# Layer 0's first expert prepared between row blocks, split rank gathers, and another memory order for layer 1

## The chip, the cores and the metric

The kernel runs on one core of one Trainium2 chip. A core has five engines with queues of their own: TensorE (PE in the profile: matrix products; PEld is its weight load), VectorE (DVE), ScalarE (ACT), GpSimd (POOL) and SyncE (SP, which here only issues transfers). They meet through semaphores. Transfers run on 16 DMA engines that all queues of the core share. The metric is the device time in microseconds (us) of one execution, as the median of several runs. All data are float32.

## The reference

The input `x` has 32 batches of 128 x 1024. Two residual layers follow each other.

```python
# layer 0
h = einsum('bct,bcd->bdt', x, weights[cond])        # weights[cond[b]]: 128 x 128, per batch
logits = h @ gate_w.T                               # 4096 tokens of 1024, 64 experts
w, sel = top_k(softmax(logits), 8); w = w / sum(w)
# token -> slot: the first 256 tokens of each expert, in token order, the rest dropped
out = (silu(xin @ wg) * (xin @ wu)) @ wd            # per expert 256 x 1024 -> 384 -> 1024
x = x + sum over the chosen experts of w * out
# layer 1
c = x @ W.T + scal[a] * (x @ A[a].T) @ Bm[a].T      # a = adapter of the batch, rank 16
logits = c @ router_w.T + router_b                  # 8 experts
gate = top 2 of softmax(logits), made to sum to 1
y = c @ base_w.T + base_b + 2 * sum_e gate_e * (c @ lora_A[e]) @ lora_B[e]
x = x + y
```

## The kernel before

**Three stages.** Stage A (0 to 200 us) makes `h`, the routing and part of a weight product. Stage B (259 to 2123 us) runs over the 64 experts. Stage C (2123 us to the end) is layer 1, over 16 pairs of batches. Between A and B and between B and C lie the row blocks of the weight product.

**Stage A.** The loop runs over the 32 batches `b`. `loaded_batch(b)` gathers the batch's matrix `w_b` (indirect DMA on GpSimd's queue) and loads `x_b` (0.5 MB, SyncE's queue); six batches are loaded ahead, in buffers of a pool with six of each. `mixed` makes `ph` (16 matmuls of 128 columns) and `as_rows` and `stored` write it as token rows to `hbuf` in DRAM. `logits` makes `plog` (16 matmuls of 64 columns, four batches to a PSUM bank), `topped`, `powers` and `weights_of` choose the eight experts and their weights. For a group of four batches, `counted(g)` makes `pcnt` (how many tokens of each batch go to each expert), adds it up over the batches in `upto` (four VectorE additions), then makes two tiles `prk` (a token's rank in its batch and its weight) that ScalarE copies and stores to `ranks` in DRAM. `plog`, `pcnt` and `prk` share a PSUM pool, `pa_sm`, with three buffers. `carried(b)` copies `x` of a batch to `ybuf` in DRAM, on SyncE's queue; after the loop it is called again for the last eight batches.

**The weight product.** Layer 1 never forms `c`: the matrix W (and the adapters' Bm) is multiplied with the head, which is lora_A, router_w and base_w side by side, 1160 columns in three blocks of 388, 388 and 384 (`BLOCKS`, n = 0, 1, 2). `combined(n, d)` or `multiplied(n, d)` makes one of nine row blocks d of a column block, `pcw`, with eight matmuls; its right factor is `hw` (`head_block(n)`), its left one of three tiles of three row blocks each (`left_block`, tiles `WB_a` and `WB_b`). These share the buffers of the experts' weights: `hw_n` those of `wg`, the `WB` tiles those of `wu` and `wd`. Row blocks 0 to 7 of n = 0 and 1 go to `cwbuf` in DRAM, block 8 to `G_sb`. n = 0 is made inside stage A, n = 1 between A and B, n = 2 between B and C.

**From ranks to tokens.** `looked_up(es)` computes, for four experts, which batch holds each of the 256 slots (`batch`, `rank`, `row`: eleven VectorE operations). `fetched(part, count)` gathers `count` rows of `ranks` into `rkg`, one indirect DMA each (two per expert). `found(part, lo, hi)` finds each slot's token and weight (`slot_tok`, `slot_w`) and `byq`; `placed` multiplies `byq` by `spread` on TensorE (`prow`, one PSUM bank in the pool `pf`) and writes `slot_row`, the rows of `hbuf`. `gathered(e)` issues eight indirect DMAs into `xin`. `columns(e)` transposes `xin` to `xT` on VectorE. `prow`'s pool has one bank, and it is not used before the row blocks of n = 1.

**Stage B.** Gate and up product of an expert are one 256 x 1024 times 1024 x 768 product in the Winograd form: seven products of half size (`product`, tile `pp`, four matmuls each) of sums of quarters (`weight_sums`: tiles t1, t2, t4 and one in place; `token_sums`: s1, s2, s4 and one in place), with their results added on VectorE (`gated`). `turned` transposes h on TensorE (`pth`, copied to `hTb`), `po` is the down product, ScalarE scales it into `o_sb`, and GpSimd scatters it with an addition into `ybuf`. The sums and the tokens of expert e + 1 are made while expert e runs.

**Passage to C and stage C.** The map `BM` (10 x 2 x 512 columns on each partition) is loaded from `cwbuf` (two of three pieces, `PIECES`), from `lora_B`, from `G_sb` and from the row blocks of n = 2. `with_ones` adds 1 on the diagonal, so that the residual x is part of the product; it compares `chan` (a row 0 to 1023) with `own`. `map_sums(lo, hi)` makes the sums ts1, ts2, ts4 for the seven-product form, `token_sums2` those of the tokens (ss1, ss2, ss4). `loaded_x1` loads a pair's tokens from `ybuf` (`xq`), which needs the last scatter; `turned_x1` transposes them on VectorE to `X`. `inner` makes `px`, the product of `X` with the first 136 columns and the adapter's columns (`pxw`); `routed`, `corrected` and `turned_in` make the expert and adapter rows of `X`. Then `pr_c` are the seven products of a pair.

**What sets the order.** The objects `dve`, `pe`, `act`, `pool` and `sync` record instructions that keep the order of the program on their engine; instructions issued through `nc.` are placed by a scheduler. Tiles of a pool with one buffer that follow another pool on the same addresses wait for the last readers of what lay there:

```python
    c1 = ctx.enter_context(tc.tile_pool(name="c1", bufs=1, reuse_waits="tile"))
    BM = c1.tile([P, KC, 2, 512], F32, name="BM")
    pxw = [c1.tile([P, HC, NA], F32, name=f"pxw_{i}") for i in range(2)]
    chan = c1.tile([P, 2, 512], F32, name="chan")
```

In this order `BM` lies over the tables of slots and the last `o_sb` tiles of stage B.

Of the kernel before, what the change touches and what calls it, by code (L numbers as in the profile page):

```python
# [51 lines left out]
def kernel(  # L52
# [273 lines left out]

    with (
# [3 lines left out]
        tc.tile_pool(name="pa_big", bufs=4, space=PSUM) as pa_big,  # L331
        tc.tile_pool(name="pa_sm", bufs=3, space=PSUM) as pa_sm,
# [3 lines left out]
        def loaded_batch(b):  # L336
# [8 lines left out]
            sync.dma_start(xs[b].rearrange("p j c -> p (j c)"), x_q[b])  # L345
# [78 lines left out]
        def counted(g):  # L424
            mask, wt = masks[g], wts_of[g]
            pcnt = pa_sm.tile([P, GB, E], F32, name=f"pcnt_{g}", tag="sm")
# [103 lines left out]
        part = {0: looked_up([0, 1, 2, 3])}  # L530
        fetched(part[0], 4 * NJ)
        for b in range(NB - 8, NB):
            carried(b)
        gathers = {}
        for d in range(HC + 1):
            step = combined(1, d)
            next(step)
            if d == 2:
                found(part[0], 0, 1)
                placed(part[0])  # L540
                gathers[0] = gathered(0)
            elif d == 3:
                found(part[0], 1, 2)
                placed(part[0])
                gathers[1] = gathered(1)
            elif d == 4:
                found(part[0], 2, 4)
                part[1] = looked_up([4, 5, 6, 7])
                fetched(part[1], 4 * NJ)
            next(step)  # L550

# [4 lines left out]
    dve.tensor_scalar(adapter_rows, adapter_i, float(P), pcol, ALU.mult, ALU.add)  # L556
    dve.tensor_copy(adapter_f, adapter_i)
    dve.tensor_tensor(
        smask,
        adapter_f.unsqueeze(2).to_broadcast([P, NB, E2]),  # L560
        iota_t[:, 0:E2].unsqueeze(1).to_broadcast([P, NB, E2]),
        ALU.is_equal,
    )
    dve.tensor_tensor(
        smask, smask, scal_bc.unsqueeze(1).to_broadcast([P, NB, E2]), ALU.mult
    )

    dve.tensor_scalar(own, iota_t[:, 0:HC], float(Q), inquad, ALU.mult, ALU.add)
    dve.tensor_scalar(far, quad, float(W4), None, ALU.mult)
    dve.tensor_scalar(own, own, far, None, ALU.add)  # L570

    nc.sync.dma_start(rb_bc, router_b.to_broadcast([P, E2]))


    with (
# [3 lines left out]
        tc.tile_pool(name="pb_s", bufs=4, space=PSUM, reuse_waits="tile") as pb_s,  # L579
        tc.tile_pool(name="pb_o", bufs=2, space=PSUM, reuse_waits="tile") as pb_o,  # L580
# [115 lines left out]

        mine = loaded(0)
        left, right = {}, {}
        for _ in weight_sums(0, *mine[:2], right):
            pass  # L700
        xT = columns(0, gathers[0])
        for _ in token_sums(0, xT, left):
            pass
        halves = gathers[1]
        p1 = first_product(0, left, right)
        for e in range(E):
# [62 lines left out]


    BM = c1.tile([P, KC, 2, 512], F32, name="BM")
    pxw = [c1.tile([P, HC, NA], F32, name=f"pxw_{i}") for i in range(2)]
    chan = c1.tile([P, 2, 512], F32, name="chan")
    nc.gpsimd.iota(
        chan.rearrange("p n c -> p (n c)"),
        pattern=[[1, H]],
        base=0,
        channel_multiplier=0,
        allow_small_or_imprecise_dtypes=True,
# [9 lines left out]
    def map_sums(lo, hi):  # L789
        b11, b12 = rows_of(0)[:, :, 0, lo:hi], rows_of(0)[:, :, 1, lo:hi]  # L790
        b21, b22 = rows_of(1)[:, :, 0, lo:hi], rows_of(1)[:, :, 1, lo:hi]
        dve.tensor_tensor(t1[:, :, lo:hi], b12, b11, ALU.subtract)
        dve.tensor_tensor(t2[:, :, lo:hi], b22, t1[:, :, lo:hi], ALU.subtract)
        dve.tensor_tensor(b12, b22, b12, ALU.subtract)
        dve.tensor_tensor(t4[:, :, lo:hi], b21, t2[:, :, lo:hi], ALU.subtract)
# [340 lines left out]
```

## Time and profile before

| | |
|---|---|
| median of 3 runs | 2758.08 us (2755.9 to 2762.82) |
| profiled execution | 2751.29 us |
| span in the profile (first to last instruction) | 2749.5 us |
| mean granted TensorE clock | 0.996 |
| TensorE busy | 2709.0 us, 8900 matmuls |
| VectorE busy | 1597.9 us |
| GpSimd busy | 1118.7 us |
| ScalarE busy | 426.6 us |
| DMA | 572.55 MB |

Times in the profile are of the one profiled execution, counted from the start of its span. A line of the timeline gives the start, the duration, the engine, the source line, the operation, output and inputs, the number of instructions merged into the line, and in brackets the idle time in front and who ended it. All operations that go through the recording objects carry line L212, so groups are told apart by their tiles. The granted clock is that of TensorE: 1.00 is full speed, 0.50 is half.

### The profile page before, as it was taken

The page shows a single profiled execution, that of the slowest core. Times are in us where ns is not written, and L with a number is a line of the kernel's source. Part 1 is how long each engine was busy: PE and PEld are TensorE (multiplying, and loading weights), DVE is VectorE, ACT ScalarE, POOL GpSimd, SP SyncE. Part 2 cuts the span into 40 slices and gives each one's busy share as a digit, 9 for nine tenths or more (in the row PEclk, how much of TensorE's full clock was granted, in tenths as well). Part 3 has the DMA queues.
Part 4 walks back from the last instruction along what each step waited for, and adds up shares of the span by engine and source line. Part 5 has one row for each costly group of instructions (what it writes and reads, how often), then busy time and mean ns, then how long its engine had stood idle before and what let it go on. Part 6 is the DMA issues. An engine that isn't in the chain of part 4 may idle for free.

```text
span 2749.5 us, 24289 instructions
## 1 busy us (share of the span) xinstructions
PE 2709.0 (99%) x8900; PEld 1522.9 (55%) x8900; DVE 1597.9 (58%) x2535; ACT 426.6 (16%) x824; POOL 1118.7 (41%) x845
## 2 busy tenths in 40 slices
PE   8998999999999999999999999999999899999999
PEld 7875555555555555555555555555555555555554
DVE  3434866757667566676667666676663544444442
ACT  2220111111111111111111111111111000000000
POOL 2106456555555556555565564655551100000000
PEclk9999999999999999999999999999999999999999
DMA  9985777777787778777787887877775532222210
GB/s 360 387 316 198 241 226 245 252 242 244 240 244 254 229 247 262 222 246 257 233 252 235 245 257 223 253 259 227 236 244 154 137 75 62 61 62 61 63 41 38
DMA packets 127430, 572.55 MB, mean 208 GB/s; under 512 B 23056, under 2 KB 49744, under 8 KB 101328
## 3 DMA queue, kind: packets, MB, share of 16 engines
q1 hardware_dynamic: 66784, 392.59, 38.8%
q0 software_dynamic: 51200, 155.24, 24.4%
q10 hardware_dynamic: 9328, 23.17, 2.2%
q8 instruction: 70, 1.15, 0.2%
q14 instruction: 48, 0.39, 0.0%
HBM read 463.87 MB, written 128.02 MB: 215 GB/s over the span
## 4 chain that ended last, share of the span: by engine, by line
PE 96%; DVE 2%; issue 1%; DMA 1%; another core or an unknown queue 0%; ACT 0%; ACTq 0%; SPq 0%; DVEq 0%
PE pp L633 41%; PE po L732 24%; PE pr_c L212 17%; PE pcw L212 4%; PE px L212 2%; PE ph L212 2%; PE plog L212 2%; PE pth L683 2%; DMA wu<-in_wu 0%; DVE upto L212 0%; DVE hit L212 0%; PE pg L212 0%; PE prk L212 0%; PE pt L212 0%
## 5 line engine op out<-in xcount | busy, mean ns | idle before, releaser
L314 POOL DMA_INDIRECT xin<-hbuf,slot_row x512 | 717.7, 1402 | 157.5 <-issue 155.4
L732 PE MATMUL po<-wd,hTb 128*128 128x512 f32 x1536 | 680.3, 592 | 0.6 <-ACT hTb L685 0.6
L743 POOL DMA_INDIRECT ybuf<-o,slot_tok x128 | 206.2, 1611 | 675.4 <-ACT o L741 468.8
L732 PEld LDWEIGHTS po<-wd,hTb 128*128 128x128 f32 x1536 | 286.8, 190 | 323.7 <-issue 306.1
L633 PE MATMUL pp<-wg,xT 128*128 128x384 f32 x1024 | 351.5, 486 | 0.0
L633 PE MATMUL pp<-t,s 128*128 128x384 f32 x1024 | 342.0, 487 | 0.0
L633 PEld LDWEIGHTS pp<-t,s 128*128 128x128 f32 x1024 | 193.4, 190 | 141.9 <-issue 23.0
L212 DVE TENSOR_TENSOR u<-p,pp 128x384 f32<-128x384 f32 x64 | 35.4, 554 | 386.0 <-PE pp L633 372.8
L633 PEld LDWEIGHTS pp<-wg,xT 128*128 128x128 f32 x1024 | 189.6, 190 | 119.0
L741 ACT ACTIVATE o<-po,slot_w 128x512 f32<-128x512 f32 x256 | 175.9, 687 | 494.2 <-PE po L732 483.7
L212 POOL DMA_INDIRECT ab<-in_AT,adapter_rows x32 | 36.5, 1140 | 443.9 <-ACT pxw L212 438.3
L212 PE MATMUL pr_c<-BM,X 128*128 128x512 f32 x480 | 213.7, 592 | 0.0
L212 DVE STREAM_TRANSPOSE xT<-xin 128x1024 f32<-128x1024 f32 x128 | 155.8, 1234 | 69.1 <-DMA xin<-hbuf,slot_row 64.8
L633 PE MATMUL pp<-t,xT 128*128 128x384 f32 x512 | 175.7, 486 | 0.1
L633 PE MATMUL pp<-wu,s 128*128 128x384 f32 x512 | 175.6, 486 | 0.0
L633 PE MATMUL pp<-wu,xT 128*128 128x384 f32 x512 | 175.6, 486 | 0.0
L650 ACT ACTIVATE h<-gate 128x384 f32<-128x384 f32 x128 | 66.9, 523 | 699.3 <-DVE gate L212 696.9
L248 POOL DMA_INDIRECT rkg<-ranks,row x128 | 125.4, 980 | 96.3 <-DMA ranks<-rk 57.6
L212 PEld LDWEIGHTS pr_c<-BM,X 128*128 128x128 f32 x480 | 88.9, 190 | 100.2 <-issue 100.0
L212 PE MATMUL pr_c<-ts,ss 128*128 128x512 f32 x320 | 142.5, 592 | 1.3 <-DVE ss L212 1.3
L212 DVE TENSOR_TENSOR u<-u,pp 128x384 f32<-128x384 f32 x128 | 70.5, 551 | 125.0 <-PE pp L633 124.9
L633 PEld LDWEIGHTS pp<-t,xT 128*128 128x128 f32 x512 | 97.2, 190 | 68.3 <-DVE u L212 0.7
(159 smaller groups left out, 2953.0 us busy)
## 6 DMA issues: line engine op xcount, KB each, us to landing
wu<-in_wu SPq DMA_DIRECT2D x64, 1536.0 KB
wg<-in_wg SPq DMA_DIRECT2D x64, 1536.0 KB
wd<-in_wd SPq DMA_DIRECT2D x64, 1536.0 KB
ybuf<-in_x SPq DMA_DIRECT2D x40, 512.0 KB
x<-in_x_q SPq DMA_DIRECT2D x32, 512.0 KB
hbuf<-hq ACTq DMA_DIRECT2D x32, 512.0 KB
xq<-ybuf SPq DMA_DIRECT2D x64, 256.0 KB
out_y<-out_c SPq DMA_DIRECT2D x32, 512.0 KB
```

The source lines that it names most:

```text
L212: return lambda *args, **kw: kept(op(*args, **kw))
L248: nc.gpsimd.indirect_dma_start(out=some["rk"][:, s, :, :].rearrange("p i t -> p (i t)"), out_offset=None, in_=ranks.rearrange("e b i t -> ...
L314: nc.gpsimd.indirect_dma_start(out=xin[:, q, :], out_offset=None, in_=quarters, in_offset=bass.IndirectOffsetOnAxis(ap=slot_row[:, s : s + ...
L633: nc.tensor.matmul(bank, left[k][:, j, :], right[k][:, j, :], start=(j == 0), stop=(j == HH - 1))
L650: nc.scalar.activation(h, gate, AF.Sigmoid)
L683: nc.tensor.transpose(pt[:, i, :], h[:, i * P : (i + 1) * P], ident)
L732: nc.tensor.matmul(po, hT[j][:, i, :], wd_sb[:, i, cols], start=(i == 0), stop=(i == IC - 1),)
L741: nc.scalar.mul(o_sb[:, cols], po, slot_w[:, s : s + 1])
L743: nc.gpsimd.indirect_dma_start(out=ybuf, out_offset=bass.IndirectOffsetOnAxis(ap=slot_tok[:, s : s + 1], axis=0), in_=o_sb, in_offset=None ...
```

## The change

Seven things change.

1. The loads of x_2 to x_5 are issued by GpSimd's queue in place of SyncE's, each behind the gather of the same batch's matrix.
2. `pcnt` lies in the bank of `prow` (pool `pf`) in place of the pool `pa_sm`.
3. The second copying of the last eight batches of x to `ybuf` is left out.
4. The first look-up is gathered in two parts of four rows (`fetched(part[0], 2 * NJ)` twice). The row blocks of n = 1 are moved into the scope of stage B's pools, and the first expert's `weight_sums`, `columns` and `token_sums` stand behind row block 3's first half. `found(2, 4)`, the look-up of experts 4 to 7 and their gathers stand behind the first expert's first product, so the `prow` of experts 2 and 3 moves from the middle of row block 4 to behind that product; the order of TensorE's other instructions is the same. The PSUM pools of stage A are closed, and those of stage B opened, after the row blocks.
5. The seven VectorE operations on the adapters' rows and masks and on `own` (now `batch_needs`) stand in row block 1 in place of after block 8.
6. In stage C `X_0` and `chan` are the first tiles of `c1`, ahead of `BM`. `chan` is made by two VectorE operations in place of a GpSimd iota, the two copies of `G_sb` into `BM` are made by VectorE in place of ScalarE, and `with_ones` and `map_sums` over the first two pieces stand ahead of the row blocks in place of after block 2. On SyncE's queue the four loads of `BM` from `cwbuf` stand first, then `hw_2`, `WB_b_0`, `lora_B`, `WB_b_1`, the two `pxw` loads, `WB_b_2` and `xq`; before it was `hw_2`, `WB_b_0`, `WB_b_1`, `pxw`, `BM`, `WB_b_2`, `lora_B`, `xq`.
7. `map_sums` becomes a generator: over the last piece, ts1 is made, then `token_sums2` of the first pair, then ts2, the sum in `BM` and ts4.

```diff
         return halves
 
 
+    ppool = ExitStack()
+    pa_big = ppool.enter_context(tc.tile_pool(name="pa_big", bufs=4, space=PSUM))
+    pa_sm = ppool.enter_context(tc.tile_pool(name="pa_sm", bufs=3, space=PSUM))
     with (
         tc.tile_pool(name="a1", bufs=1) as a1,
         tc.tile_pool(name="a6", bufs=6) as a6,
         tc.tile_pool(name="a2", bufs=2) as a2,
-        tc.tile_pool(name="pa_big", bufs=4, space=PSUM) as pa_big,
-        tc.tile_pool(name="pa_sm", bufs=3, space=PSUM) as pa_sm,
     ):
         xs, ws, hTs, hqs, plogs, tops, lefts_of, exs, masks, wts_of = ({} for _ in range(10))
 
...
                 in_offset=bass.IndirectOffsetOnAxis(ap=cond_rows[:, b : b + 1], axis=0),
             )
             xs[b] = a6.tile([P, HC, P], F32, name=f"x_{b}", tag="x_q")
-            sync.dma_start(xs[b].rearrange("p j c -> p (j c)"), x_q[b])
+            queue = pool if 2 <= b < 6 else sync
+            queue.dma_start(xs[b].rearrange("p j c -> p (j c)"), x_q[b])
 
         def carried(b):
             sync.dma_start(ybuf[b * P : (b + 1) * P, :], x[b])
...
 
         def counted(g):
             mask, wt = masks[g], wts_of[g]
-            pcnt = pa_sm.tile([P, GB, E], F32, name=f"pcnt_{g}", tag="sm")
+            pcnt = pf.tile([P, 512], F32, name=f"pcnt_{g}", tag="prow")
+            pcnt = pcnt[:, 0 : GB * E].rearrange("p (t e) -> p t e", t=GB)
             pe.matmul(pcnt, ones, mask, start=True, stop=True)
             for t in range(GB):
                 b = g * GB + t
...
         weights_of(NB // GB - 1)
         some_rows()
         counted(NB // GB - 1)
-        part = {0: looked_up([0, 1, 2, 3])}
-        fetched(part[0], 4 * NJ)
-        for b in range(NB - 8, NB):
-            carried(b)
-        gathers = {}
-        for d in range(HC + 1):
-            step = combined(1, d)
-            next(step)
-            if d == 2:
-                found(part[0], 0, 1)
-                placed(part[0])
-                gathers[0] = gathered(0)
-            elif d == 3:
-                found(part[0], 1, 2)
-                placed(part[0])
-                gathers[1] = gathered(1)
-            elif d == 4:
-                found(part[0], 2, 4)
-                part[1] = looked_up([4, 5, 6, 7])
-                fetched(part[1], 4 * NJ)
-            next(step)
-
+    part = {0: looked_up([0, 1, 2, 3])}
+    fetched(part[0], 2 * NJ)
 
 
     nc.sync.dma_start(adapter_i, adapter.to_broadcast([P, NB]))
     nc.sync.dma_start(scal_bc, scal.to_broadcast([P, E2]))
...
     nc.sync.dma_start(rb_bc, router_b.to_broadcast([P, E2]))
+
+    def batch_needs():
+
+
+        dve.tensor_scalar(adapter_rows, adapter_i, float(P), pcol, ALU.mult, ALU.add)
...
+        dve.tensor_scalar(own, own, far, None, ALU.add)
 
 
     with (
         tc.tile_pool(name="b1", bufs=1, reuse_waits="tile") as b1,
         tc.tile_pool(name="b2", bufs=2, reuse_waits="tile") as b2,
         tc.tile_pool(name="b3", bufs=3, reuse_waits="tile") as b3,
-        tc.tile_pool(name="pb_s", bufs=4, space=PSUM, reuse_waits="tile") as pb_s,
-        tc.tile_pool(name="pb_o", bufs=2, space=PSUM, reuse_waits="tile") as pb_o,
+        ExitStack() as bpool,
     ):
         def columns(e, halves):
             xT = b2.tile([P, HC, CAP], F32, name=f"xT_{e}", tag="xT")
...
             place[4 * k - 3] = k
             look[max(4 * k - 10, 0)] = k
 
+
         mine = loaded(0)
         left, right = {}, {}
-        for _ in weight_sums(0, *mine[:2], right):
-            pass
-        xT = columns(0, gathers[0])
-        for _ in token_sums(0, xT, left):
-            pass
-        halves = gathers[1]
+        for d in range(HC + 1):
+            step = combined(1, d)
+            next(step)
+            if d == 1:
+                batch_needs()
+            elif d == 2:
+                found(part[0], 0, 1)
+                placed(part[0])
+                xin = gathered(0)
+            elif d == 3:
+                fetched(part[0], 2 * NJ)
+                found(part[0], 1, 2)
+                for _ in weight_sums(0, *mine[:2], right):
+                    pass
+                placed(part[0])
+                halves = gathered(1)
+                xT = columns(0, xin)
+                for _ in token_sums(0, xT, left):
+                    pass
+            next(step)
+        ppool.close()
+        pb_s = bpool.enter_context(
+            tc.tile_pool(name="pb_s", bufs=4, space=PSUM, reuse_waits="tile")
+        )
+        pb_o = bpool.enter_context(
+            tc.tile_pool(name="pb_o", bufs=2, space=PSUM, reuse_waits="tile")
+        )
         p1 = first_product(0, left, right)
+        found(part[0], 2, 4)
+        part[1] = looked_up([4, 5, 6, 7])
+        fetched(part[1], 4 * NJ)
         for e in range(E):
             wd_sb = mine[2]
             following = ({}, {})
...
     pc_t = ctx.enter_context(tc.tile_pool(name="pc_t", bufs=2, space=PSUM, reuse_waits="tile"))
 
 
+    X0 = c1.tile([P, KC, 2 * P], F32, name="X_0", tag="X")
+    chan = c1.tile([P, 2, 512], F32, name="chan")
+
 
     BM = c1.tile([P, KC, 2, 512], F32, name="BM")
     pxw = [c1.tile([P, HC, NA], F32, name=f"pxw_{i}") for i in range(2)]
-    chan = c1.tile([P, 2, 512], F32, name="chan")
-    nc.gpsimd.iota(
-        chan.rearrange("p n c -> p (n c)"),
-        pattern=[[1, H]],
-        base=0,
-        channel_multiplier=0,
-        allow_small_or_imprecise_dtypes=True,
+    step = c1.tile([P, HC], F32, name="step")
+    dve.tensor_scalar(step, iota_t[:, 0:HC], float(P), None, ALU.mult)
+    dve.tensor_tensor(
+        chan.rearrange("p n (k c) -> p (n k) c", c=P),
+        iota_t.unsqueeze(1).to_broadcast([P, HC, P]),
+        step.unsqueeze(2).to_broadcast([P, HC, P]),
+        ALU.add,
     )
 
 
...
     def map_sums(lo, hi):
         b11, b12 = rows_of(0)[:, :, 0, lo:hi], rows_of(0)[:, :, 1, lo:hi]
         b21, b22 = rows_of(1)[:, :, 0, lo:hi], rows_of(1)[:, :, 1, lo:hi]
-        dve.tensor_tensor(t1[:, :, lo:hi], b12, b11, ALU.subtract)
+        yield dve.tensor_tensor(t1[:, :, lo:hi], b12, b11, ALU.subtract)
         dve.tensor_tensor(t2[:, :, lo:hi], b22, t1[:, :, lo:hi], ALU.subtract)
         dve.tensor_tensor(b12, b22, b12, ALU.subtract)
-        dve.tensor_tensor(t4[:, :, lo:hi], b21, t2[:, :, lo:hi], ALU.subtract)
+        yield dve.tensor_tensor(t4[:, :, lo:hi], b21, t2[:, :, lo:hi], ALU.subtract)
 
     right = {
         1: rows_of(0)[:, :, 0, :],
...
         return ab
 
     def turned_x1(q, xq, side):
-        X = side.tile([P, KC, 2 * P], F32, name=f"X_{q}", tag="X", bufs=1)
+        X = X0 if q == 0 else side.tile([P, KC, 2 * P], F32, name=f"X_{q}", tag="X", bufs=1)
         for t in range(2):
             dve.transpose(
                 X[:, 0:HC, t * P : (t + 1) * P].rearrange("p j (q r) -> p q j r", r=Q),
...
         return {1: a11, 2: a12, 3: s4, 4: a22, 5: s1, 6: s2, 7: a21}
 
 
-    hw = head_block(2)
-    lefts = left_block("b", 0, "wu") + left_block("b", 1, "wd")
-    for i in range(2):
-        nc.sync.dma_start(pxw[i][:, :, 0:NX], cwbuf[:, :, 0:NX])
     at = NX
     for lo, hi in PIECES[0:2]:
         for n in range(2):
-            nc.sync.dma_start(BM[:, 0:HC, n, lo:hi], cwbuf[:, :, at : at + hi - lo])
+            sync.dma_start(BM[:, 0:HC, n, lo:hi], cwbuf[:, :, at : at + hi - lo])
             at += hi - lo
+    hw = head_block(2)
+    lefts = left_block("b", 0, "wu")
+    sync.dma_start(BM[:, HC, :, :].rearrange("p n c -> p (n c)"), lora_B)
+    lefts += left_block("b", 1, "wd")
+    for i in range(2):
+        sync.dma_start(pxw[i][:, :, 0:NX], cwbuf[:, :, 0:NX])
     lefts += left_block("b", 2, "wd")
-    nc.sync.dma_start(BM[:, HC, :, :].rearrange("p n c -> p (n c)"), lora_B)
+    xq = loaded_x1(0, c1)
+    ab = own_maps(0)
+
+    first = PIECES[2][0]
     at = NX
     for lo, hi in PIECES[0:2]:
-        act.copy(
+        dve.tensor_copy(
             BM[:, HC + 1, :, lo:hi],
             G_sb[:, at : at + 2 * (hi - lo)].rearrange("p (n c) -> p n c", n=2),
         )
         at += 2 * (hi - lo)
-    xq = loaded_x1(0, c1)
-    ab = own_maps(0)
-
-    first = PIECES[2][0]
-    last = None
+    for c in range(HC):
+        with_ones(c, 0, first, BM[:, c, :, 0:first])
+    for _ in map_sums(0, first):
+        pass
     for d in range(HC + 1):
         _, pcw = multiplied(2, d, hw, lefts, pc_p, "pp", pe)
         pcw = pcw.rearrange("p (n c) -> p n c", n=2)
...
             with_ones(d, first, 512, pcw)
         else:
             act.copy(BM[:, HC + 1, :, first:512], pcw)
-        if d == 2:
-            for c in range(HC):
-                with_ones(c, 0, first, BM[:, c, :, 0:first])
-            map_sums(0, first)
-        elif d == 3:
+        if d == 3:
             X = turned_x1(0, xq, c1)
         elif d == 4:
             pxs, xm = inner(0, X, ab)
...
             mid = routed(0, pxs, corrected(0, X, pxs))
         elif d == 7:
             turned_in(0, X, HC, mid)
-    map_sums(first, 512)
+    sums = map_sums(first, 512)
+    next(sums)
     left = token_sums2(0, X)
+    next(sums)
 
     wpool.close()
     c3 = ctx.enter_context(tc.tile_pool(name="c3", bufs=1, side="right", reuse_waits="tile"))
```

More of the change, by code (lines that the diff above doesn't have):

```diff
@@ L554 @@
+    fetched(part[0], 2 * NJ)
     nc.sync.dma_start(adapter_i, adapter.to_broadcast([P, NB]))
     nc.sync.dma_start(scal_bc, scal.to_broadcast([P, E2]))
[L556 to L566, printed above, removed]
@@ L568 @@
-    dve.tensor_scalar(own, iota_t[:, 0:HC], float(Q), inquad, ALU.mult, ALU.add)
-    dve.tensor_scalar(far, quad, float(W4), None, ALU.mult)
-    dve.tensor_scalar(own, own, far, None, ALU.add)
-    nc.sync.dma_start(rb_bc, router_b.to_broadcast([P, E2]))
+    nc.sync.dma_start(rb_bc, router_b.to_broadcast([P, E2]))
+    def batch_needs():
+        dve.tensor_scalar(adapter_rows, adapter_i, float(P), pcol, ALU.mult, ALU.add)
+        dve.tensor_copy(adapter_f, adapter_i)
+        dve.tensor_tensor(
+            smask,
+            adapter_f.unsqueeze(2).to_broadcast([P, NB, E2]),
+            iota_t[:, 0:E2].unsqueeze(1).to_broadcast([P, NB, E2]),
+            ALU.is_equal,
+        )
+        dve.tensor_tensor(
+            smask, smask, scal_bc.unsqueeze(1).to_broadcast([P, NB, E2]), ALU.mult
+        )
+        dve.tensor_scalar(own, iota_t[:, 0:HC], float(Q), inquad, ALU.mult, ALU.add)
+        dve.tensor_scalar(far, quad, float(W4), None, ALU.mult)
+        dve.tensor_scalar(own, own, far, None, ALU.add)
@@ L698 @@
         left, right = {}, {}
-        for _ in weight_sums(0, *mine[:2], right):
-            pass
-        xT = columns(0, gathers[0])
-        for _ in token_sums(0, xT, left):
-            pass
-        halves = gathers[1]
+        for d in range(HC + 1):
[21 more added lines that the diff above has]
+            tc.tile_pool(name="pb_s", bufs=4, space=PSUM, reuse_waits="tile")
+        )
+        pb_o = bpool.enter_context(
+            tc.tile_pool(name="pb_o", bufs=2, space=PSUM, reuse_waits="tile")
+        )
         p1 = first_product(0, left, right)
+        found(part[0], 2, 4)
+        part[1] = looked_up([4, 5, 6, 7])
+        fetched(part[1], 4 * NJ)
         for e in range(E):
@@ L767 @@
     pc_t = ctx.enter_context(tc.tile_pool(name="pc_t", bufs=2, space=PSUM, reuse_waits="tile"))
+    X0 = c1.tile([P, KC, 2 * P], F32, name="X_0", tag="X")
+    chan = c1.tile([P, 2, 512], F32, name="chan")
     BM = c1.tile([P, KC, 2, 512], F32, name="BM")
     pxw = [c1.tile([P, HC, NA], F32, name=f"pxw_{i}") for i in range(2)]
[L773 to L779 removed]
+    step = c1.tile([P, HC], F32, name="step")
+    dve.tensor_scalar(step, iota_t[:, 0:HC], float(P), None, ALU.mult)
+    dve.tensor_tensor(
+        chan.rearrange("p n (k c) -> p (n k) c", c=P),
+        iota_t.unsqueeze(1).to_broadcast([P, HC, P]),
+        step.unsqueeze(2).to_broadcast([P, HC, P]),
+        ALU.add,
     )
```

## The prediction

> **What bounds the kernel now.** I read the page's busy shares first, then the granted clock by slices, then TensorE's waits, then the timelines of TensorE, VectorE, GpSimd and SyncE around each wait.
>
> ```profile
> PE 2709.0 (99%) x8900; PEld 1522.9 (55%) x8900; DVE 1597.9 (58%) x2535; ACT 426.6 (16%) x824; POOL 1118.7 (41%) x845
> PE   8998999999999999999999999999999899999999
> ```
>
> The second line is TensorE's busy share in 40 slices of 68.7 us. TensorE is busy for 2709.0 of 2749.5 us, so whatever moves other engines' work can gain at most the 40.5 us of idle time and the matmuls that ran at half clock after it. Slices 1, 4 and 32 are the weak ones: the start, the passage to the experts, the passage to the second layer. TensorE's waits name them (total, times, longest, in us):
>
> ```profile
> PE ph L212 <- DMA w<-in_cond_w,cond_rows: 10.6, 1, 10.6
> PE px L212 <- issue: 9.8, 1, 9.8
> PE prow L212 <- DVE byq L212: 7.8, 2, 7.5
> PE prk L212 <- DVE upto L212: 3.4, 7, 1.3
> PE pth L683 <- DVE h L212: 1.4, 1, 1.4
> PE pr_c L212 <- DVE ss L212: 1.3, 1, 1.3
> ```
>
> Between the passages an expert takes 29.0 us and TensorE has no gap, so the 64 experts are not touched by any of this. Windows over the two passages (TensorE, its weight loads, VectorE, ScalarE, GpSimd busy; then granted clock, DMA share, GB/s) show the second price of a long wait:
>
> ```profile
> 228.00:238.00 10.00, 5.54 (x10) 3.29 (x11) 9.38 (x31) 0.48 (x1) 7.54 (x8) 0.50 0.33 99
> 238.00:259.00 21.00, 21.00 (x65) 12.22 (x64) 13.29 (x13) 1.93 (x4) 16.73 (x15) 0.99 0.61 204
> 2149.00:2166.00 17.00, 7.20 (x36) 6.89 (x36) 11.35 (x11) 0.39 (x1) 0.00 (x0) 0.70 0.54 102
> ```
>
> After the 7.5 us wait the clock granted is 0.50, after the 9.8 us wait it averages 0.70: row-block matmuls then start 0.646 us apart instead of 0.326. About 8 ran so in the first place (8 x 0.32 = 2.7 us lost) and the first of the px group in the second (2.4 us).
>
> **Start.** The first product waits for w_0, an indirect gather that GpSimd issues at 5.00 us (1.11 us long) behind six x loads of 0.5 MB and the router's 0.25 MB from SyncE. Those 3.25 MB at the 0.42 MB/us seen from 4 us on need until about 11.5, and w_0 lands among them at 10.6. The change takes x_2 to x_5 off SyncE and puts each on GpSimd behind its own w, so at 6 us only 1.25 MB lie ahead: 4 + 1.25/0.42 = 7.0, plus part of w_0's and w_1's 0.13 MB, and 1.9 us, which is what a later, undisturbed gather (rkg, issue ends 208.75, first reader 210.68) needs from issue to landing. I take 8.3 us, a gain of 2.3. The trace has no direct DMA issued by GpSimd; its neighbours are SyncE's x issue (2.74/5 = 0.55 us) and GpSimd's indirect issue (0.95 + 0.30 us). Taken at 1.25 like the latter, x_2 is issued near 9 and x_5 near 16; a batch needs 3.6 us of TensorE, so batch 2 is due near 13, batch 5 near 27. Bounds: no gain if the transfers share the engines so that w_0 lands as before; 4 us if w_0 lands 1.9 us after 5.00 + 1.11, less a little.
> The Trainium skill, "DMA: Bandwidth & Descriptors", section "Issuing engines are not separate DMA queues", says that transfers run on the same 16 engines and interleave whoever issues them, so issuing from another engine saves only issue time. By that rule alone this edit would be worth nothing; what it leaves is the later issue of four loads, which is what I count.
>
> **Counts.** The second rank product of a group waits for the bank of the counts, and so for four additions on VectorE (upto). Putting the counts in a bank of another pool leaves it waiting only for a copy long done. I find seven stalls of about 0.5 us and one of 1.5 (at 166.6 us): 4.5 us by the gaps beyond the normal start distance, 3.4 by the waits table. I take 4.5. Between 40 and 80 us the DMA share is 1.02, so a faster TensorE might have to wait for loads instead: bound 0 to 5.4 (with the 0.7 us wait of plog).
>
> **Eight copies of x to ybuf dropped.** They are repeats at the end of the first stage (151 to 179 us on SyncE) and nothing waits there: the next load, wg, is held until 198.2 by the buffer of the row blocks' right factor. Cost and gain zero; it frees 8 x 1 MB of traffic.
>
> **First passage.** Before, expert 2 and 3's place in the look-up (found, 4.4 us of VectorE) came in front of a small product, prow, that stood in the middle of a row block, and VectorE reached it late:
>
> ```profile
> 227.83 0.23 DVE L212 TENSOR_SCALAR slot_row<-prow,qrow 128x8 int32<-128x8 f32 x1 [10.08 <-remote]
> 232.46 0.61 PE L212 MATMUL prow<-byq,spread 128*128 128x16 f32 x2 [7.53 <-DVE byq L212]
> 232.91 26.39 PE L212 MATMUL pcw<-hw,WB_a 128*128 128x388 f32 x72
> 259.13 2.74 PE L633 MATMUL pp<-wg,xT 128*128 128x384 f32 x8
> ```
>
> After, that prow stands behind expert 0's first product, so nothing of TensorE's order before it depends on it. TensorE goes from 219.47 through 88 block matmuls at 0.326 us: 248.2 instead of 259.1. What must be ready by then: weight sums (4 x 1.76 us on VectorE, from 217.6: wu_0 was loaded at 84, wg_0 lands near 205), xT_0 and its sums (2.4 + 4 x 0.7). xin_0's eight gathers now follow four rank gathers instead of eight: 214.7 to 224.7, landed near 226.5; xT_0 by 229, sums by 233. The second prow needs found(2,4): about 237. So there are over 10 us of slack, also if slot_row is as late (227.8) as before. ScalarE's copies of blocks 3 and 4 were late too (230.7, 242.9) and the blocks that reuse their banks come at 237.7 and 243: that is narrow. The seven small operations of batch_needs (235.3 to 237.0, 1.7 us) move into VectorE's 7.84 us wait for the first rkg, which hides them; without that cover found(0,1) and all behind it come 1.7 us later, inside the slack. Expert 1's weights move forward with the last block, so the 1.4 us wait of pth stays. Gain 7.5 + 0.2 + 2.7 = 10.4; bounds 5 (half of it back as another late event) to 11.
>
> **Second passage.** px waits for X, the transposed tokens, which VectorE reaches only after eight with_ones on BM (6.46 us) and four sums (7.3 us), and these wait for BM's load, which waits until the last scatter has freed the memory that BM lies on:
>
> ```profile
> 2131.94 4.09 SPq L963 DMA_DIRECT2D BM<-cwbuf  x4
> 2143.50 6.46 DVE L212 SCALAR_TENSOR_TENSOR BM<-chan,own,BM 128x640 f32<-128x640 f32 x8 [4.09 <-DMA BM<-cwbuf]
> 2158.87 6.61 PE L212 MATMUL px<-pxw,X 128*128 128x152 f32 x32 [9.80 <-issue]
> ```
>
> After, X_0 and chan lie there, and BM lies on memory whose last readers are the last expert's products and sums (about 2101), so its load is 30 us earlier. VectorE then has chan and two copies of G_sb (both its own now: near 1.3 us, as a 128x1024 add goes by the 0.69 us of 128x512, and some 0.8 each), with_ones and sums done by about 2130 to 2133, the four block pieces at 2128 to 2144, and X when xq has landed (its source is complete at 2131.9, as before) at about 2147 to 2149; px is due at 2148.9. Gain 9.8 + 2.4 + 0.3 = 12.5, of which I leave 0.7 for a rest of the wait.
> The price is on SyncE: the loads of hw_2 and WB_b_0, which TensorE needs at 2123.1, were issued at 2077 and 2080, and now stand behind BM's four, on the same queue, held by the same 2101. BM's 2.56 MB took 11.6 us from issue with other traffic and 9.2 at its rate; the scatter of the expert before takes some 2.9 us of DMA time; hw_2 and WB_b_0, 1.54 MB each, 3.8 us apiece at 0.41 MB/us. 2101.5 + 1 + 9.2 + 2.9 + 7.6 = 2122.2, 2124.6 with 11.6. I take a wait of 1.5; bounds 0 and 6, or 11 where the wait is long enough to halve the clock.
> pr_c's wait of 1.3 us goes: the token sums now stand before three of the four sums that kept them (4 x 1.15 us). I take 1.4 with the start distance.
>
> **Sum.** 2.3 + 4.5 + 10.4 + 12.5 + 1.4 - 0.7 - 1.5 = 28.9 us. The profiled execution took 2751.3 us (span 2749.5), so it would be 2722.4; the median of the runs shown, 2758.1, lies 6.8 above it, and I forecast against the median: 2729.2.
>
> **Rivals.** *Heads late (0.17).* hw_2 and WB_b_0 land at 2128 or later: 5 us or more of wait and up to 5.1 us of half clock (10.24 us at 0.50, as after 228): 9 to 11 of the 28.9 return, 2738 to 2740. For it: 5.6 MB must pass in 21.6 us. Against: the queue had nothing from 2108 to 2120.
> *First passage not healed (0.13).* Between 218 and 260 us VectorE and ScalarE act on TensorE's signals up to 8 us after the matmul's recorded end (slot_row above, "remote"). If the copies of blocks 3 and 4 stay that late and the clock halves once, 8 to 10 us return: 2737 to 2739.
> *BM still held by the last scatter (0.04).* Then hw_2 and WB_b_0 are issued at 2136 and land near 2151: TensorE idle 28 us and cold, 33 lost for 13.9 gained; the total gain is nil, 2754 to 2762: the change would not do what its reordered memory promises.
> *Slower (0.08).* The late signals of 218 to 260 us last into the expert loop, because the look-up of experts 4 to 7 and 16 gathers now meet experts 0 and 1. From 0.6 us per expert this eats the gain (64 x 0.6 = 38 us), at 1 us per expert it gives 2793. For it: hTb came 0.6 us late once at 2111. Against: no such signal later than 260 us.
>
> **How the numbers follow.** The forecast has 0.58, and with terms at their bounds runs from 2718 (start 4, counts 5.4, no new waits, runs a few us off the median) to 2736 (start and counts nothing). Reaching to the heads and the first passage gives 2718 to 2745; left out are nil gain and slower, and part of the tails. About 0.3% (8.3 us) is what a measurement of this kernel can tell from no change: faster 0.88, same 0.04, slower 0.08.
>
> **What would show it.** In the profile after: first ph at 8 to 9 us; no prk wait on upto; clock 1.00 through 200 to 260 us and the first pp near 240 (all earlier gains in); BM's load before hw_2's; px without a wait or under 2 us; a pcw wait on hw or WB_b of about 1.5 us; 29.0 us per expert. It would be wrong if pcw's first block waits over 5 us, if xT_0 or byq holds TensorE, or if an expert takes longer.

## The result and the profile after

The changed kernel takes 2735.76 us (median of five, 2735.58 to 2736.00); the kernel before took 2761.58 us beside it (five, 2755.90 to 2762.82). The ratio is 0.9912 (0.9898 to 0.9927), 25.8 us faster. The two profiled executions, 2751.29 and 2735.81 us, lie only 15.5 us apart, since the profiled execution of the kernel before was faster than all its timed ones. The forecast, 2729.2 (2718 to 2745), holds the time. The runs below show that three of its terms (start, counts, first passage) are nevertheless not what was gained.

The page after has the busy shares and TensorE's row of 40 slices. Slice 4 and slice 32 are full now; slice 1 is not.

```profile
PE 2705.5 (99%) x8900; PEld 1521.7 (56%) x8900; DVE 1601.5 (59%) x2539; ACT 427.1 (16%) x822; POOL 1117.5 (41%) x848
PE   8999999999999999999999999999999999999999
```

TensorE's longest waits after (total, times, longest, in us):

```profile
PE ph L212 <- DMA w<-in_cond_w,cond_rows: 9.0, 1, 9.0
PE prk L212 <- DVE wt L212: 6.1, 2, 6.0
PE pp L618 <- ACT G_sb L212: 5.1, 1, 5.1
```

The waits of px (9.8), of pr_c (1.3) and of prow on byq (7.5 at the longest) are gone, and so are those of prk on upto. Two waits are new, and they say where a part of the sum went: 6.0 us of prk on wt, the weights of the chosen experts, and 5.1 us of the first expert's second product on a copy by ScalarE. TensorE's timeline at the two places, then the window of the second passage:

```profile
167.41 0.69 PE L212 MATMUL prk<-order,wt 128*64 128x128 f32 x2 [5.95 <-DVE wt L212]
...
221.35 28.92 PE L212 MATMUL pcw<-hw,WB_a 128*128 128x388 f32 x88
250.11 2.74 PE L618 MATMUL pp<-wg,xT 128*128 128x384 f32 x8
252.69 0.29 PE L212 MATMUL prow<-byq,spread 128*128 128x16 f32 x2
258.05 7.07 PE L618 MATMUL pp<-t,s 128*128 128x384 f32 x16 [5.07 <-ACT G_sb L212]
```

```profile
2147.00:2166.00 19.00, 19.00 (x83) 13.13 (x82) 4.71 (x21) 2.54 (x5) 0.00 (x0) 1.00 0.67 139
```

The 88 row-block matmuls run without a gap, as forecast; the wait that ended them is replaced by one two groups of instructions later. After it 16 matmuls take 7.07 us, the first of them at half clock, where the same 16 take 5.32 in the kernel before. In the second passage TensorE is busy for all 19 us at clock 1.00.

For comparing runs, this table gives three marks of each profiled execution, taken from the starts of TensorE's instructions: the first matmul of row block 0 of n = 1, the time from there to the first expert's second product (the passage to the experts), and the time from the first row block of n = 2 to the first pr_c (the passage to layer 1). The last column is the median of all executions of that kernel. The stretch from the second expert's first product to the row blocks of n = 2 is 1845.5 us wherever it was compared (both first profiles, both second ones, u_start, late), so the experts' loop is untouched.

| kernel | chip | row blocks of n = 1 begin | passage to experts | passage to layer 1 | median, us |
|---|---|---|---|---|---|
| before, first profile | first | 200.4 | 61.3 | 63.8 | 2761.6 |
| changed, first profile | first | 202.3 | 55.8 | 51.5 | 2735.8 |
| before_again | 12 | 206.1 | 50.6 | 65.2 | 2744.5 |
| after_again | 12 | 202.0 | 50.8 | 51.5 | 2729.3 |
| u_start | 5 | 201.8 | 50.5 | 51.5 | 2728.1 |
| u_counts | 5 | 208.5 | 50.5 | 51.5 | 2731.0 |
| u_stage | 5 | 201.7 | 50.5 | 64.1 | 2742.4 |
| u_passage | 5 | 203.5 | 50.7 | 51.5 | 2729.4 |
| late | 12 | 201.9 | 50.8 | 51.5 | 2728.2 |
| late_counts | 12 | 208.1 | 50.6 | 52.4 | 2732.0 |
| late_start | 12 | 202.0 | 50.6 | 51.5 | 2729.2 |
| u_memory | 12 | 202.8 | 50.6 | 54.7, begun 29 us late | 2761.3 |
| act_copies | 12 | 195.9 | 52.0 | 51.5 | 2722.7 |
| act_banks | 3 | 194.2 | 60.7 | 51.5 | 2729.5 |

Runs fell on several chips. The kernel before took 2743.5 us beside the runs on chip 5, 2743.5 to 2744.8 on chip 12, 2754.4 on chip 3: times are compared within a chip, or between 5 and 12, which agree. One execution of the kernel before on chip 12 took 5860.5 us and is left out.

### The profile page after: what moved, and what is told of

It reads as the page before. It is cut to its first block, busy times and chain, and to the rows that moved or that the text cites. A ratio compares the mean times of both kernels' runs of the same rounds, so it can differ in the third digit from the quotient of the medians.

```text
span 2734.0 us, 24269 instructions
## 1 busy us (share of the span) xinstructions
PE 2705.5 (99%) x8900; PEld 1521.7 (56%) x8900; DVE 1601.5 (59%) x2539; ACT 427.1 (16%) x822; POOL 1117.5 (41%) x848
## 4 chain that ended last, share of the span: by engine, by line
PE 94%; DMA 2%; DVE 1%; issue 1%; another core or an unknown queue 1%; ACT 0%; SPq 0%; ACTq 0%; DVEq 0%
PE pp L618 42%; PE po L742 24%; PE pr_c L212 18%; PE pcw L212 3%; PE px L212 2%; PE ph L212 2%; PE pth L668 2%; PE plog L212 1%; DMA hw<-in_head_w 1%; DMA hbuf<-zeros 1%; PE prk L212 0%; DMA wu<-in_wu 0%; DMA x<-in_x_q 0%; PE pg L212 0%
```

## The experiments

**Each part undone.** Two theories: the first stage ends when its transfers let it, so that time gained before 160 us is only waited for at 161; or each term adds, as in the sum. For the passages: the old order costs what the first profile showed, or late signals cost it.

u_start:

```diff
-            queue = pool if 2 <= b < 6 else sync
-            queue.dma_start(xs[b].rearrange("p j c -> p (j c)"), x_q[b])
+            sync.dma_start(xs[b].rearrange("p j c -> p (j c)"), x_q[b])
```

> The changed kernel (2735.8 us) with the loads of x_2 to x_5 back on SyncE's queue. Theory 'transfers set the end of the first stage' (the transfers of 40 to 160 us, at a DMA share of 1.02, set when the stall at 161 us ends, so that time gained earlier is only waited for there): TensorE starts 1.6 us later, at 10.6, and the end moves by 0 to 0.6 us: 2735.5 to 2736.4. Rival 'each term adds' (the prediction's sum): the start's 1.7 us come back in full, 2737.5.

Measured: 2728.07 us (2726.77 to 2728.69). The first product starts at 11.47, the 6 us stall shrinks to 4.3, and the row blocks begin at 201.8 as in the changed kernel (202.0). The start's gain is waited away; nothing is lost by undoing it.

u_counts:

```diff
-            pcnt = pf.tile([P, 512], F32, name=f"pcnt_{g}", tag="prow")
-            pcnt = pcnt[:, 0 : GB * E].rearrange("p (t e) -> p t e", t=GB)
+            pcnt = pa_sm.tile([P, GB, E], F32, name=f"pcnt_{g}", tag="sm")
```

> The changed kernel with the counts back in the pool of the logits and ranks. Theory 'transfers set the end of the first stage': seven stalls of 0.5 us return before 160 us, the stall at 161 us (6.1 us now) shrinks by as much, and the end moves by 0 to 1 us: 2735.5 to 2737. Rival 'each term adds': 4.5 us return, 2740.3.

Measured: 2731.01 us, with a spread of 2726.52 to 2735.02; the profiled execution is the 2735.02. Waits of prk on upto return with 5.0 us in all, and the row blocks begin at 208.5. So neither theory holds fully: the profiled one is 6 us later, the fastest not at all. What goes with the difference is the granted clock: the four executions, fastest first, had a mean clock of 1.000, 0.999, 0.998 and 0.997. In the profiled one TensorE runs at half clock in three stretches ahead of the row blocks, which begin at or just after waits of 1.8, 1.9 and 0.7 us. Windows of u_counts over them (columns as in the prediction):

```profile
43.80:47.21 3.41, 3.41 (x11) 2.15 (x10) 0.63 (x1) 0.58 (x1) 0.00 (x0) 0.50 1.01 416
170.10:176.93 6.83, 6.35 (x29) 6.05 (x30) 1.45 (x3) 1.75 (x3) 0.00 (x0) 0.50 0.35 106
187.20:194.03 6.83, 6.83 (x29) 5.85 (x28) 3.42 (x12) 0.95 (x2) 0.00 (x0) 0.50 0.05 11
```

TensorE is busy there for 16.6 us at half clock; in the changed kernel's second profile it is 3.6 us, in one stretch. Matmuls take about twice as long then, so half of the 13.0 us between them is lost: 6.5 us, an estimate, and as much as the whole difference between 208.5 and 202.0.

u_stage (all behind the experts as before):

> The changed kernel with everything behind the experts as before (memory order, SyncE's order, chan, the copies, the place of the sums). Both theories: the 9.8 us wait of px, its half clock (2.4 to 2.7) and the 1.3 to 1.5 us wait of pr_c return: 13.8 us by the two profiles, 2749.6. Under 12 us would mean that part of what the passage gains is from something else, over 15 that the old order costs more than its profile showed.

Measured: 2742.41 us (2741.76 to 2744.09), 13 to 14.3 us above u_passage and u_start of the same chip. It is within 1.1 us of the kernel before there (ratio 0.9998, 0.9988 to 1.0007). On this chip the second passage is nearly the whole gain.

u_passage (the row blocks in their old scope, one fetch of eight rows, `found(2, 4)` in row block 4, the seven operations of `batch_needs` behind block 8):

> The changed kernel with the passage to the experts as before (first expert's sums behind the row blocks, found(2,4) in front of its prow in row block 4, one fetch of eight rows). Theory 'late signals take their share': the changed passage loses 5.3 us waiting plus 1.6 at half clock, the old one 7.7 + 2.7 + 0.2, so 3.7 us return, 2739.5; more, up to 2750, if the spread of the kernel before (2755.9 to 2762.8) is made in this passage. Rival 'each term adds': 10.4 us return, 2746.2, with little spread.

Measured: 2729.39 us (2728.68 to 2729.93), and the wait of 7 us is not in its profile, although the order is the old one. TensorE's waits of u_passage:

```profile
PE ph L212 <- DMA w<-in_cond_w,cond_rows: 9.0, 1, 9.0
PE prk L212 <- DVE wt L212: 6.4, 2, 6.1
...
PE prow L212 <- DVE byq L212: 0.4, 2, 0.2
```

The old order does not cost 10.4 us, nor the 3.7 of the other theory, on this chip.

**Both kernels again.** This asked for the same two kernels where the late signals are absent.

> The changed kernel itself, for comparison on the same chip, since the kernel before took 2743.5 us there in place of 2761.6. If late TensorE signals in the passage to the experts are what the two places differ in (none of the last four profiles shows one), the changed kernel loses its 5.3 us wait and 1.6 us of half clock: 2728 to 2729.5. If the other place is slower throughout by 0.65%, it takes 2718.

Measured: 2729.31 us (2728.47 to 2730.54; ratio 0.9947, 0.9929 to 0.9965). The wait of pp on G_sb is gone, the stall at 161 is not (6.2 us).

> The kernel before itself, for a second profile of it, on a chip where it takes 2741 to 2748 us. Theory 'the 7.5 us wait of prow was made by late TensorE signals, not by the order': without them prow of experts 2 and 3 waits under 0.5 us, the clock stays 1.00 from 200 to 260 us, and the profiled execution takes 2751.3 - 7.7 - 2.7 = 2740.9. Rival 'the order itself costs it' (the prediction): the wait of 7 to 8 us and the half clock stand there as in the first profile, and the time differs elsewhere.

Measured: 2744.53 us (2744.01 to 2748.17). The 2740.9 was missed, since the first stage ran slower (row blocks at 206.1) and the second passage took 65.2 us in place of 63.8, but the wait is settled: its longest on byq is 0.2 us, and the clock is 1.00 from 200 to 260 us. The profiled execution was the slowest of the ten. Its first stage has 10.2 us at half clock (3.41 from 170.9 and 6.83 from 184.6), the first profile of the same kernel none; half of that is 5.1 of the 5.7 us between 206.1 and 200.4. VectorE's and TensorE's timelines of the kernel before, second profile:

```profile
225.33 0.23 DVE L212 TENSOR_SCALAR slot_row<-prow,qrow 128x8 int32<-128x8 f32 x1 [2.11 <-PE prow L212]
```

```profile
230.44 0.29 PE L212 MATMUL prow<-byq,spread 128*128 128x16 f32 x2
230.59 23.71 PE L212 MATMUL pcw<-hw,WB_a 128*128 128x388 f32 x72
```

prow of the second expert is issued at 225.01 and slot_row follows it at 225.33, once prow has ended; in the first profile it came 8.2 us after prow's end. With signals on time, byq is there before TensorE asks for it, and the passage takes 50.6 us in the old order and 50.8 in the new.

**What holds the first stage.** The changed kernel's ScalarE and VectorE, first profile, ahead of the new wait:

```profile
154.00 0.48 ACT L212 COPY cw<-pcw 128x388 f32<-128x388 f32 x1 [2.47 <-DMA hbuf<-hq]
163.16 0.32 ACTq L212 DMA_DIRECT2D cwbuf<-cw  x1
163.53 1.08 ACT L212 COPY hT<-ph 128x512 f32<-128x512 f32 x2 [9.04 <-DMA hbuf<-zeros]
...
164.84 0.93 ACT L212 ACTIVATE ex<-plog,nmax 128x64 f32<-128x64 f32 x4 [0.24 <-issue]
```

```profile
165.81 0.43 DVE L212 TENSOR_TENSOR wt<-ex,mask 128x256 f32<-128x256 f32 x1 [8.17 <-ACT ex L212]
```

ScalarE has copied a row block by 154.5 and cannot issue its store until 163.2: the issue waits for the store of zeros, issued at 146.4, to land. That takes 16.7 us. Meanwhile SyncE issues seven copies of x to ybuf, between 145.7 and 156.9, and the DMA share is 1.03 to 1.05 from 140 to 160 us. Behind the issue stand the copies of ph and the exponentials, and behind these wt and prk. That the copies of x are what holds the zeros is the theory; four runs move them.

late:

```diff
-            for _ in range(2 if b in (12, 16, 20, 24) else int(b >= 4)):
+            if 4 <= b < 22:
                 carried(next(copies))
...
         counted(NB // GB - 1)
+        for b in copies:
+            carried(b)
```

> The changed kernel with the copies of x to ybuf of 14 of the 32 batches moved behind the last count of the first stage (about 165 to 200 us), where the DMA share is 0.0 to 0.7. Theory 'transfers set the end of the first stage': the store of zeros that holds ScalarE at 163 us lands early, the stall of 6 us at 161 us and its half clock (1.2 us) go: 6 to 7.5 us faster than the changed kernel of the same chip, with no prk wait over 1 us. Rival: the exponentials are late for another reason (ScalarE's own order), and no more than 1 us changes; or the moved copies delay wg and wd and 1 to 5 us are lost behind 200 us.

Measured: 2728.20 us (2727.28 to 2728.79), only 1.1 us less. The stall at 161 falls to 0.9, and another comes at 175. TensorE's and SyncE's timelines of late:

```profile
162.81 0.43 PE L212 MATMUL prk<-order,wt 128*64 128x128 f32 x2 [0.88 <-DVE wt L212]
179.09 3.22 PE L212 MATMUL plog<-gw_sb,hT 128*128 128x64 f32 x14 [3.68 <-DVE left L212]
```

```profile
143.82 27.95 SPq L212 DMA_DIRECT2D ybuf<-in_x  x14
```

The copies were put later in the program, but SyncE has nothing to wait for there: it issues them from 143.8, as soon as the last x is issued. The zeros, issued at 143.88, still take 15.0 us until ScalarE can go on at 158.90. Then ScalarE is held until 177 instead of 163, waiting for a store of hq that was issued while these copies ran (6.59 us idle).

late_counts:

> As the run with moved copies, and the counts back in the pool of the logits and ranks. If transfers hid the gain of the counts' edit, it shows here: seven to eight stalls of 0.5 us, 3.5 to 4.5 us slower than with moved copies alone. Rival: the stalls are made good by waits elsewhere, under 1 us.

Measured: 2731.95 us (2728.95 to 2735.65), 3.8 us above late, the row blocks at 208.1 in place of 201.9. Between the medians the counts' edit is worth 3.8 of the forecast 4.5 us here; between the fastest executions of the two it is 1.7. The profiled execution is again the slowest and has 13.6 us of TensorE's work at half clock ahead of the row blocks, late has 7.9; half of the difference is 2.8 of the 6.2 us between their row blocks.

late_start:

> As the run with moved copies, and x_2 to x_5 back on SyncE's queue. If transfers hid the gain of the start, it shows here: first product at 10.6 to 11.5 in place of 9.0, 1.6 to 2.5 us slower than with moved copies alone. Rival: the first 160 us stay bound by transfers and under 0.6 us shows.

Measured: 2729.15 us (2727.47 to 2729.74), 1.0 us above late with overlapping spreads, the row blocks at 202.0 against 201.9. The first product is 1.65 us later (10.57) and the end of the stage is not.

act_copies:

```diff
-            for _ in range(2 if b in (12, 16, 20, 24) else int(b >= 4)):
+            if 4 <= b < 28:
                 carried(next(copies))
...
             next(step)
+            if d > 0:
+                b = next(copies)
+                act.dma_start(ybuf[b * P : (b + 1) * P, :], x[b])
```

> The changed kernel with eight of the 32 copies of x to ybuf issued by ScalarE behind its copies of row blocks 0 to 7 (205 to 250 us), so that they cannot run ahead as those moved on SyncE's queue did. Theory 'transfers hold ScalarE's queue near 160 us': 8 MB of traffic less before 165 us (19 us of transfer time at 0.42 MB/us), the stall of 6 us at 161 us and the one of 3.8 us that moved to 175 us both go, 5 to 7 us faster than the changed kernel: 2722 to 2724 where that takes 2729. Rival: ScalarE's order or the loads of x hold it anyway, within 1 us of 2729; or the copies delay wd_0 and xin, 1 to 4 us slower.

Measured: 2722.65 us (2721.83 to 2724.01; ratio to the kernel before 0.9922, 0.9904 to 0.9939), 6.7 us faster than the changed kernel on the same chip. Windows of after_again, then of act_copies (TensorE, weight loads, VectorE, ScalarE, GpSimd busy, clock, DMA share, GB/s):

```profile
140.00:165.00 25.00, 21.75 (x160) 18.83 (x158) 5.87 (x16) 4.71 (x9) 0.94 (x1) 0.99 0.96 370
165.00:200.00 35.00, 31.30 (x194) 25.77 (x194) 16.01 (x50) 10.34 (x27) 0.00 (x0) 0.91 0.31 113
```

```profile
140.00:165.00 25.00, 25.00 (x189) 22.15 (x188) 11.36 (x31) 8.22 (x17) 0.95 (x1) 1.00 0.83 312
165.00:200.00 35.00, 34.26 (x199) 26.85 (x198) 16.19 (x59) 8.56 (x20) 0.00 (x0) 0.95 0.37 128
```

ScalarE waits for a row block ahead of each copy, so these eight cannot run ahead; the DMA share before 165 us falls from 0.96 to 0.83 and TensorE has no gap there. The zeros are issued at 146.56, as before, and ScalarE issues the row block's store at 154.71, right behind its copy, 8.1 us later in place of 16.7. So the copies did hold that queue. The row blocks begin 6.1 us earlier. The price is 1.2 us in the passage, where the first prow waits 1.6 us for slot_tok.

**The second passage by itself.** u_memory keeps the order of the loads and gives the tiles their old places:

```diff
-    X0 = c1.tile([P, KC, 2 * P], F32, name="X_0", tag="X")
-    chan = c1.tile([P, 2, 512], F32, name="chan")
...
     pxw = [c1.tile([P, HC, NA], F32, name=f"pxw_{i}") for i in range(2)]
+    chan = c1.tile([P, 2, 512], F32, name="chan")
...
-        X = X0 if q == 0 else side.tile([P, KC, 2 * P], F32, name=f"X_{q}", tag="X", bufs=1)
+        X = side.tile([P, KC, 2 * P], F32, name=f"X_{q}", tag="X", bufs=1)
```

> The changed kernel with its order of loads on SyncE's queue, but BM, pxw and chan first in memory and X_0 last, as before. Theory 'the memory order is what lets BM load early': BM's load waits for the last o tiles again, hw_2 and WB_b_0 stand behind it, TensorE is idle from its last down product for 20 to 28 us and then at half clock for up to 10 us (5 lost): 25 to 33 us slower than the changed kernel, 2754 to 2762 on a chip where that takes 2729. Rival 'the order of VectorE's work is enough': under 3 us slower.

Measured: 2761.34 us (2759.77 to 2761.57; ratio 1.0062, 1.0044 to 1.0080), 32.0 us above after_again. SyncE's queue of u_memory, then its first row block, then SyncE's queue of the changed kernel:

```profile
2124.56 4.21 SPq L212 DMA_DIRECT2D BM<-cwbuf  x4
2128.89 2.02 SPq L212 DMA_DIRECT2D hw<-in_head_w  x1
2131.01 2.50 SPq L212 DMA_DIRECT2D WB_b<-in_WB  x1
```

```profile
2143.93 16.32 PE L212 MATMUL pcw<-hw,WB_b 128*128 128x384 f32 x41 [28.32 <-DMA WB_b<-in_WB]
```

```profile
2099.65 5.32 SPq L212 DMA_DIRECT2D BM<-cwbuf  x4
2105.02 1.86 SPq L212 DMA_DIRECT2D hw<-in_head_w  x1
2106.92 2.33 SPq L212 DMA_DIRECT2D WB_b<-in_WB  x1
```

The new order on SyncE's queue pays only with the new memory order. In the old places BM's load is issued 9 us after TensorE is ready for the row blocks (at 2115.6), in the changed kernel 22 us before it is (at 2121.6), and the heads behind it keep TensorE idle for 28.3 us: a forecast rival's mechanism (28 us, 33 with the half clock) is real, and the memory order is what keeps it out.

**A bank for the late copy.** On top of act_copies:

```diff
-            halves = multiplied(n, d, hws[n], lefts, pa_big, "big", pe)
+            other = (n, d) == (1, HC)
+            place, tag = (pa_sm, "sm") if other else (pa_big, "big")
+            halves = multiplied(n, d, hws[n], lefts, place, tag, pe)
```

> The run with eight copies on ScalarE's queue, and row block 8 of n = 1 in a bank of the logits' pool, so that no bank of the first expert's products waits for ScalarE's copy of it. On a chip whose profile of the kernel before shows no wait in the passage to the experts: 2722 to 2724, as without the bank (under 0.5 us between them), since nothing waits for that copy. On a place where TensorE's signals come late at the passage (first profile of the changed kernel: 5.3 us of wait and 1.6 at half clock): about 7 us faster than without the bank if the late copy hurts through the bank alone; no gain if the signals stay held as long as TensorE runs.

Measured, on a chip where the kernel before takes 2754.4 us: 2729.48 us (2723.47 to 2732.79; ratio 0.9906, 0.9888 to 0.9924). The late signals are there, and the passage takes 60.7 us with the bank. ScalarE's and TensorE's timelines:

```profile
249.72 0.48 ACT L212 COPY cw<-pcw 128x388 f32<-128x388 f32 x1 [15.94 <-remote]
...
251.26 0.48 ACT L212 COPY G_sb<-pcw 128x388 f32<-128x388 f32 x1 [1.07 <-remote]
```

```profile
250.25 4.67 PE L620 MATMUL pp<-wg,xT 128*128 128x384 f32 x8 [6.56 <-issue]
```

Now it is the copy of row block 7 that comes 11 us after that block's last matmul, and the first product, which takes that block's bank, waits for it. Whether the bank is worth anything without the lateness of block 7 is not told, as no kernel without it ran on that chip.

## Why the prediction was right, and where it was not

**Second passage: right, a little too small.** "Gain 9.8 + 2.4 + 0.3 = 12.5, of which I leave 0.7", less a new wait of 1.5, and 1.4 for pr_c: 11.7 us. Both deductions were zero: BM's load is issued at 2099.7, and the first row block follows the last down product without a wait. The profiles give 63.8 - 51.5 = 12.3 and 1.7 behind the first pr_c, so 14.0; u_stage gives 13 to 14.3.

**First passage: the step that failed.** "Gain 7.5 + 0.2 + 2.7 = 10.4; bounds 5 to 11." The wait was read as a cost of the order, where the first profile itself marked VectorE's idle time as "remote", 8.2 us after the product that should have ended it. (8 x 0.32 is 2.6; 72 matmuls took 26.39 us in place of 23.71, so the 2.7 is right as measured.) With signals on time the old order costs nothing (before_again, u_passage), below the stated bound. Where signals come late, both orders pay: 61.3 against 55.8 us on the first chip. Of these 5.5 us, 2.1 are lost again behind the mark, where the second product starts at half clock (from the second product to the second expert's first one it is 17.98 us in place of 15.85), so 3.4 of the 10.4 stayed. The rival "first passage not healed" described what happened there, ScalarE's late copy and the half clock included; the place it named was block 3 or 4, and it was block 8. Its ground "no such signal later than 260 us" was misread: in the first profile of the kernel before, ScalarE's copy of the first product at 264.08 is marked "remote" too.

**Counts and start: the terms that transfers took.** "I take 4.5" and "I take 8.3 us, a gain of 2.3". The first product came at 8.96, 1.65 us earlier, and the seven stalls went. But the stage ended at 202.3 in the first profile, 1.8 us later than before: the 6.0 us stall at 161 took all of it. On chip 12 the stage is 4.1 us shorter than before (206.1 to 202.0), but the profile of the kernel before there is its slowest execution, 3.6 us above the median, with 5.1 us lost at half clock. By the medians, 1.1 us is what u_stage, which has all the earlier edits, gains on the kernel before. So of 6.8 us forecast next to nothing arrived. The values taken were wrong although the DMA share of 1.02 stood beside them, and the half clock in this stage, 6.83 us long in both profiles of the changed kernel, was in no term. The start's upper bound of 4 does not follow from its own numbers either: 10.6 - (5.00 + 1.11 + 1.9) is 2.6. u_start and late_start say the start's part is at most 1 us; u_counts and late_counts that the counts' part is 1.7 to 3.8 us in the medians, and by their profiles much of it is time lost at half clock.
The rule of the Trainium skill, "DMA: Bandwidth & Descriptors", section "Issuing engines are not separate DMA queues", that issuing from several engines saves only the time to issue, fits the end of the stage (201.8 and 202.0). The first product did come 1.65 to 2.6 us earlier; that this is due to the later issue of the four loads, as the prediction counted it, is argued, since no run issues them later on SyncE's own queue.

**Copies dropped: nothing against it.** They were counted at nothing, and wg is still loaded at 200.0 (198.2 before); no run puts them back alone.

**The total.** 28.9 us were forecast. Between the first profiles it is 15.5, on chip 12 it is 15.2 (2744.5 to 2729.3), between the medians on the first chip 25.8. By the first profiles the terms are -1.8 for start and counts (6.8 forecast), 3.4 for the first passage (10.4) and 14.0 for the second (11.7). The medians lie further apart because the kernel before ran 4.6 to 11.5 us longer in its other executions there than in its profiled one, while the changed kernel stayed within 0.4 us. That 25.8 comes near to 28.9 is therefore luck. That late signals of varying length make this spread is argued, not shown: those executions have no profile here.

## What to carry to other kernels

A wait whose releaser had long finished need not be a property of the order: look at how long after its producer's end the waiting instruction starts, and profile the kernel a second time, on another chip, before putting such a wait into a sum. In a stage whose DMA share is 1.0, count gains on TensorE at nothing until it is clear which transfer ends last, and look for the engine whose queue holds both copies and stores: one late landing there stops everything behind it. A copy moved later in the program moves later in time only if its engine has something to wait for there; put behind row blocks on ScalarE's queue, eight copies gave 6.7 us, the fastest version here.

## What the hardware showed beside that

- On the first chip and on chip 3, TensorE's semaphore updates came up to 11 us after the modelled end of their matmuls, between 215 and 265 us only; in the eleven profiles on chips 5 and 12 ScalarE's copies of these row blocks start 0.04 us after the matmul's end, every one. In the changed kernel's first profile three updates, due at 250.3 to 253.0, came at 257.50 to 257.63. In it and in act_banks they came 2.7 and 1.6 us after GpSimd's train of gathers ended, but on chip 12 a longer train ran without late updates, and in the first profile of the kernel before some came while a train ran. The cause is open; a version with the second look-up's gathers issued later was not tried.
- A direct load issued by GpSimd takes 0.6 us and adds no wait in front of it, so that a gather and a load came every 1.9 us where 2.5 were assumed.
- Stretches at half clock that ended inside the kernel were 3.41, 6.83, 10.24, 13.65 (before_again) or, around the 28.3 us of idleness in u_memory, 30.72 us long: whole multiples of one length. They went on for 3.3 to 7.9 us after the last wait had ended, also where that wait was under 2 us (u_counts). The Trainium skill, "TensorE: Matmul & The Clock Gate", section "Part 1: The HAM clock gate", gives 3413 ns for the window over which TensorE's activity is watched, and the lengths above are multiples of it.
